# Layer 0's experts: the fifth block of 128 slots in groups of four slices, behind a jump on TensorE

## The chip, the cores and the metric

The kernel runs on one core of a Trainium2 chip. The metric is the device time of one execution in microseconds (us). A core has TensorE (PE, matrix products; its weight loads are shown as PEld), VectorE (DVE), ScalarE (ACT), GpSimd (POOL) and SyncE (SP), which run at the same time and wait for each other by semaphores. Here SP issues the plain DMA transfers and POOL the indirect ones (gathers and scatters).

## The reference

Two layers, each an attention followed by a mixture of experts, on 2048 tokens of 512 numbers. The change lies in layer 0's experts alone:

```
E, K = (NUM_EXPERTS, TOP_K)                       # 8, 2
C = math.ceil(CAPACITY_FACTOR * S * K / E)        # ceil(1.25 * 2048 * 2 / 8) = 640
probs = jax.nn.softmax(xr @ Wg, axis=-1)
gate_vals, expert_idx = jax.lax.top_k(probs, K)
...
dispatched = xr[dispatch_mask.reshape(-1) % S].reshape(E, C, d)
h = jax.nn.relu(jnp.einsum('ecd,edf->ecf', dispatched, w1))
expert_out = jnp.einsum('ecf,efd->ecd', h, w2)
```

Each of 8 experts has 640 slots. A token goes to two experts, so an expert gets 512 tokens on average, and how many it gets is known only when the router has run. An expert multiplies its slots by w1 (512 x 2048), takes the relu, and multiplies by w2 (2048 x 512). The rows go back to their tokens with their weights and are added.

## The kernel before

The program runs in stages: layer 0's attention with its router, layer 0's experts, layer 1's attention with its router, layer 1's experts. All matrix products are of 32-bit floats.

**The experts' stage** (`Experts0`). The 640 slots of an expert are five blocks of 128 (`NBLK0`), the 2048 inner columns are 16 slices of 128 (`SLICES`). `fetch` gathers a block's token rows from DRAM on POOL (g), `turn` transposes them on TensorE (tr) and copies them on DVE into xT, the expert's tokens with the 512 features on the partitions. Both are done one expert ahead, a block every two slices. Slots without a token gather some row, have the weight zero, and are scattered to rows behind the table.

For each slice, `first` computes h = w1 slice x tokens: two halves of 320 slots, each four products of 128x320 that add up in one PSUM bank (h0, h1), then a relu into hT, on ACT for the first half and on DVE for the second. `second` multiplies hT's five blocks by the slice's rows of w2, and adds them to five PSUM banks (o0 to o4) over the 16 slices. At the last slice `result` takes each o with its slots' weight into y (even blocks on ACT, odd ones on DVE), and POOL scatters y with an addition into x_dram.

`run` sets the order: for each slice `first` of this slice, then `second` of the slice before, so that the relu runs while TensorE does other products. Then come the next expert's fetch and turn, and one piece of work for layer 1 (`extra`: rope tables, and weights to load).

`weights` loads a pair of slices' w1 and w2, 512 KB each, on SP, with three buffers for each.

The compute engines keep the program's order inside this stage (`Engines`, `InOrder`); SP's transfers are placed by the framework's scheduler. The profile gives nearly all of these instructions the line of the recording helper, L65, so they are told apart by their tiles. The tiles w1 and w2 are both called w there.

[...]

## Time and profile before

| | |
|---|---|
| median of 3 runs | 3962.63 us (3961.39 to 3962.63) |
| the profiled execution | 3962.43 us |
| its span, first to last instruction | 3960.7 us |
| TensorE busy in the span | 3762.5 us |
| layer 0's experts, first h to last o on TensorE | 1413.3 to 2536.4 us |
| TensorE idle between that stage and layer 1 | 31.2 us |

In lines of groups, the part before the bar gives engine, operation, result and operands, shape and count; behind it stand busy time in all and mean duration of one, then the engine's idle time just before these instructions and what ended it. A product of 32-bit floats leaves two matmul records and two weight loads, a transpose one of each. Timeline lines give start, length and the merged instructions, in brackets the idle time before them and what ended it.

### The profile page before, as it was taken

The numbers are of one execution on the slowest core, as the hardware profiler recorded it, in microseconds if no ns is written. First come the engines' busy times: TensorE is split into PE (matmuls) and PEld (weight loads), VectorE is DVE, ScalarE is ACT, GpSimd is POOL, SyncE is SP. The second block draws the span as 40 slices with busy tenths as digits, with TensorE's granted clock in tenths as the row PEclk, the third lists the DMA queues.
The fourth block names the chain that finished last, engine by engine and source line by source line (L and its number), as shares of the span: only waits on it lengthen the run. The fifth ranks groups of instructions, "written<-read, shape, count | busy, mean of one in ns | idle before, by whom it ended". The sixth has DMA issues, their size and how long they took to land. (4 is left out here: it accounts for less than half of the span.)

```text
span 3960.7 us, 44119 instructions
## 1 busy us (share of the span) xinstructions
PE 3762.5 (95%) x14481; PEld 2417.1 (61%) x14481; DVE 1873.6 (47%) x4335; ACT 1369.1 (35%) x5089; POOL 1205.3 (30%) x1488
## 2 busy tenths in 40 slices
PE   5999899899999889999999999699999999997998
PEld 3776677688788755555555555355555555554565
DVE  7878877777788823100000000055555555553111
ACT  4665555566766401000000000043443433341111
POOL 7446655644522123111011000042222222220332
PEclk8999999899999989999999999899999999998999
DMA  5223332322322253233233232200000100005433
GB/s 170 90 94 117 115 105 95 120 91 96 115 81 81 72 191 99 93 90 82 61 91 85 65 85 72 57 22 25 28 31 22 31 22 29 18 11 207 75 65 56
DMA packets 134818, 312.45 MB, mean 79 GB/s; under 512 B 15872, under 2 KB 16000, under 8 KB 132800
## 3 DMA queue, kind: packets, MB, share of 16 engines
q1 hardware_dynamic: 116896, 268.21, 20.8%
q0 software_dynamic: 17696, 41.43, 5.7%
q8 instruction: 117, 1.92, 0.2%
q14 instruction: 109, 0.89, 0.1%
HBM read 231.72 MB, written 77.86 MB: 78 GB/s over the span
## 5 line engine op out<-in xcount | busy, mean ns | idle before, releaser
L65 PE MATMUL h<-xT,w 128*128 128x320 f32 x2048 | 574.8, 434 | 4.1 <-ACT hT L65 4.1
L65 PE MATMUL o<-w,hT 128*128 128x512 f32 x1280 | 570.0, 592 | 0.0
L65 PEld LDWEIGHTS h<-xT,w 128*128 128x128 f32 x2048 | 387.9, 191 | 191.1 <-issue 43.7
L65 DVE TENSOR_SCALAR hT<-h 128x320 f32<-128x320 f32 x128 | 62.9, 492 | 784.4 <-PE h L65 776.3
L65 PEld LDWEIGHTS o<-w,hT 128*128 128x128 f32 x1280 | 243.2, 190 | 265.5 <-issue 245.1
L65 ACT ACTIVATE hT<-h 128x320 f32<-128x320 f32 x128 | 55.8, 436 | 923.0 <-PE h L65 923.0
L65 POOL DMA_INDIRECT x_dram<-y,e_target x40 | 62.8, 1571 | 867.3 <-ACT y L65 717.4
L65 ACT ACTIVATE p<-sc,sm_nm 128x128 f32<-128x128 f32 (+1 forms) x768 | 300.9, 408 | 25.0 <-DVE sm_nm L65 14.4
L65 PE MATMUL mm<-w,xq 128*128 128x512 f32 x1024 | 294.6, 432 | 14.4 <-ACT raw L65 7.6
L65 PE MATMUL po<-w,cq 128*128 128x512 f32 x1024 | 274.2, 410 | 6.3 <-DVE cq L65 6.3
L65 PE MATMUL sc<-kT,qT 128*128 128x128 f32 (+1 forms) x1536 | 266.8, 310 | 5.9 <-ACT p L65 5.9
L65 PEld LDWEIGHTS sc<-kT,qT 128*128 128x128 f32 x1536 | 222.6, 191 | 63.2 <-issue 45.7
L65 PE MATMUL pv<-pT,v 128*128 128x256 f32 (+1 forms) x768 | 257.7, 459 | 1.4 <-ACT pT L65 1.4
L65 ACT ACTIVATE hn_sq<-mm 128x128 f32<-128x128 f32 x768 | 213.3, 278 | 121.1 <-PE mm L65 102.0
L65 DVE TENSOR_REDUCE sm_nm<-sc 128x4 f32<-128x512 f32 (+1 forms) x256 | 176.0, 687 | 140.6 <-PE sc L65 138.9
L65 PEld LDWEIGHTS mm<-w,xq 128*128 128x128 f32 x1024 | 198.8, 200 | 60.0 <-ACT raw L65 8.4
L65 PE MATMUL po<-c_wo,oT 128*128 128x512 f32 x512 | 231.4, 595 | 0.0
L65 PE MATMUL mm<-c_wq,hT 128*128 128x512 f32 x512 | 230.4, 593 | 0.4 <-DVE qn L65 0.4
L65 PEld LDWEIGHTS po<-w,cq 128*128 128x128 f32 x1024 | 185.7, 191 | 42.8 <-DVE cq L65 7.2
L65 POOL TENSOR_TENSOR hn_rs<-hn_rs,mhalf 128x4 f32<-128x4 f32 x192 | 197.2, 1027 | 16.0
L65 ACT ACTIVATE rms_sq<-mm 128x128 f32<-128x128 f32 x384 | 106.8, 278 | 273.2 <-PE mm L65 227.2
L65 PE MATMUL h<-e_w,xT 128*128 (+1 forms) x624 | 199.1, 462 | 1.7 <-DVE xT L65 1.7
(213 smaller groups left out, 6241.8 us busy)
## 6 DMA issues: line engine op xcount, KB each, us to landing
w<-in_f_w SPq DMA_DIRECT2D x128, 512.0 KB, 3.7
x_dram<-xr SPq DMA_DIRECT2D x64, 256.0 KB, 2.0
xr<-x_dram SPq DMA_DIRECT2D x64, 256.0 KB, 2.9
e_w<-in_f_w SPq DMA_DIRECT2D x8, 1408.0 KB, 22.3
xk<-in_ctxT SPq DMA_DIRECT2D x32, 256.0 KB, 2.8
xv<-in_ctxT SPq DMA_DIRECT2D x32, 256.0 KB, 3.3
raw<-in_wproj SPq DMA_DIRECT2D x32, 256.0 KB, 3.0
lnT<-kept_lnT SPq DMA_DIRECT2D x32, 256.0 KB, 3.2
```

Of the source, the lines that this page charges most:

```text
L65: return self.tc.keep_in_program_order(call(*args, **kwargs))
```

## The change

The fifth block of every expert is taken out of `first` and `second`. These now handle 512 slots: `first` makes four products of 128x512 into one bank (h), with one relu on ACT; `second` makes four products into o0 to o3.

The fifth block is done in `last`, for four slices at a time, inside a `Switch` on TensorE. For each expert TensorE has a register: 1 if slot 512 of the expert holds a token, else 0. All eight are read at the stage's start. Where it is 1, TensorE computes the block's h for the four slices of a group (hl, one bank) and the o products of the group before (ol, one bank). Where it is 0, it jumps over them. The relu of hl (rest, on DVE) and the result of ol are done either way, on what the bank holds; an empty block's weights are zero. There are five switches to an expert: four groups, and one for the last group's o products.

w1 now has 4 buffers and w2 has 6. The PSUM banks are h, hl, ol, o0 to o3 and the transposes.

In the built program the switches stand earlier than the source has them: group 0's is beside the switch that closes the expert before, inside slice 13 of that expert, and those of groups 1, 2 and 3 are inside slices 1, 7 and 11, in most experts.

```diff
     SLICES = FF0 // P
+    GROUP = 4
+    FULL = NBLK0 - 1
...
+        self.h_last = ops.t(psum, [P, self.GROUP, P], F32, "hl")
+        self.o_last = ops.t(psum, [P, D], F32, "ol")
+        ops.nc.vector.memset(self.h_last, 0.0)
+        ops.nc.vector.memset(self.o_last, 0.0)
+
+        used = ops.t(work, [P, E], I32, "used")
+        last = self.table[:, :P].rearrange("p (e b) -> p e b", e=E)[:, :, self.FULL]
+        ops.nc.vector.tensor_scalar(used, last, 0.0, None, ALU.is_gt)
+        loads, self.used = self.plain.values_load_multi_w_load_instructions(
+            used[0:1, :], engines=(mybir.EngineType.PE,), min_val=0, max_val=1,
...
-        w1 = t(self.work, [P, NC, 256], F32, "w1", 3)
+        w1 = t(self.work, [P, NC, 256], F32, "w1", 4)
...
-        w2 = t(self.work, [P, 2, D], F32, "w2", 3)
+        w2 = t(self.work, [P, 2, D], F32, "w2", 6)
...
     def first(self, e, k):
+        n = self.FULL * P
...
+        ps = self.ops.t(self.psum, [P, n], F32, "h")
+        self.inner(ps, e, k, slice(0, n))
+        hT = self.h[e, k] = self.ops.t(self.work, [P, n], F32, "hT", 3)
+        self.ops.nc.scalar.activation(hT, ps, AF.Relu)
...
+    def last(self, e, group, before):
+        g = self.GROUP
+        for arm in self.tc.Switch({mybir.EngineType.PE: self.used[e]}, 2):
+            if arm:
+                if before is not None:
+                    for i in range(g):
+                        self.outer(self.o_last, e, before * g + i, self.rest[e, before][:, i, :])
+                if group is not None:
+                    for i in range(g):
+                        s = slice(self.FULL * P, CAP)
+                        self.inner(self.h_last[:, i, :], e, group * g + i, s)
+        if group is not None:
+            rest = self.rest[e, group] = self.ops.t(self.work, [P, g, P], F32, "rest", 2)
+            self.ops.nc.vector.tensor_scalar(rest, self.h_last, 0.0, None, ALU.max)
+        else:
+            self.result(e, self.FULL, self.o_last)
...
             self.first(e, k)
             if i:
                 self.second(*steps[i - 1])
+            group, at = divmod(k, self.GROUP)
+            if at == self.GROUP - 1:
+                self.last(e, group, group - 1 if group else None)
+            if e and k == 0:
+                self.last(e - 1, None, groups - 1)
...
         self.second(*steps[-1])
+        self.last(E - 1, None, groups - 1)
```

`inner` holds the four products of `first` and `outer` the one product of `second`, on the slots they are given.

More of the change, by code (lines that the diff above doesn't have):

```diff
@@ L954 @@
     SLICES = FF0 // P
+    GROUP = 4
+    FULL = NBLK0 - 1
     def __init__(self, ops, tc, args, router, x_dram, sum_dram, work, psum):
+        self.plain, self.tc = ops.nc, tc
+        ops.nc = Engines(tc, ops.nc)
         self.ops, self.args, self.work, self.psum = ops, args, work, psum
@@ L961, in __init__ @@
         rows_behind(ops, work, sum_dram)
-        self.xT, self.g, self.w, self.h, self.outs = {}, {}, {}, {}, {}
+        self.xT, self.g, self.w, self.h, self.rest, self.outs = {}, {}, {}, {}, {}, {}
+        self.h_last = ops.t(psum, [P, self.GROUP, P], F32, "hl")
[7 more added lines that the diff above has]
+            used[0:1, :], engines=(mybir.EngineType.PE,), min_val=0, max_val=1,
+            skip_runtime_bounds_check_because="it is the result of a comparison",
+        )
+        for i in loads:
+            tc.keep_in_program_order(i)
     def column(self, e, b):
@@ L979, in weights, with inner @@
         nc, t = self.ops.nc, self.ops.t
-        w1 = t(self.work, [P, NC, 256], F32, "w1", 3)
+        w1 = t(self.work, [P, NC, 256], F32, "w1", 4)
         nc.sync.dma_start(out=w1, in_=self.args["f0_w1"][e, f])
-        w2 = t(self.work, [P, 2, D], F32, "w2", 3)
+        w2 = t(self.work, [P, 2, D], F32, "w2", 6)
         nc.sync.dma_start(out=w2, in_=self.args["f0_w2"][e, f])
         self.w[e, f] = w1, w2
+    def inner(self, ps, e, k, s):
+        w1, at = self.w[e, k // 2][0], k % 2 * P
+        for c in range(NC):
+            self.ops.nc.tensor.matmul(
+                ps, w1[:, c, at : at + P], self.xT[e][:, c, s],
+                start=(c == 0), stop=(c == NC - 1),
+            )
@@ L986, in first, with outer @@
+    def outer(self, out, e, k, hT):
+        w2 = self.w[e, k // 2][1]
+        self.ops.nc.tensor.matmul(
+            out, hT, w2[:, k % 2, :], start=(k == 0), stop=(k == self.SLICES - 1)
+        )
     def first(self, e, k):
-        nc, t = self.ops.nc, self.ops.t
+        n = self.FULL * P
         if k % 2 == 0:
             self.weights(e, k // 2)
-        w1, at = self.w[e, k // 2][0], k % 2 * P
-        hT = self.h[e, k] = t(self.work, [P, CAP], F32, "hT", 3)
-        half = CAP // 2
@@ L993, in first @@
-        for i in range(2):
-            s = slice(i * half, i * half + half)
-            ps = t(self.psum, [P, half], F32, f"h{i}")
-            for c in range(NC):
-                nc.tensor.matmul(
-                    ps, w1[:, c, at : at + P], self.xT[e][:, c, s],
-                    start=(c == 0), stop=(c == NC - 1),
-                )
-            if i:
-                nc.vector.tensor_scalar(hT[:, s], ps, 0.0, None, ALU.max)
-            else:
-                nc.scalar.activation(hT[:, s], ps, AF.Relu)
+        ps = self.ops.t(self.psum, [P, n], F32, "h")
@@ L1006, in second @@
+        self.inner(ps, e, k, slice(0, n))
+        hT = self.h[e, k] = self.ops.t(self.work, [P, n], F32, "hT", 3)
+        self.ops.nc.scalar.activation(hT, ps, AF.Relu)
     def second(self, e, k):
-        nc, t = self.ops.nc, self.ops.t
         if k == 0:
-            self.outs[e] = [t(self.psum, [P, D], F32, f"o{b}") for b in range(NBLK0)]
-        hT, w2 = self.h.pop((e, k)), self.w[e, k // 2][1]
-        for b in range(NBLK0):
-            nc.tensor.matmul(
-                self.outs[e][b], hT[:, b * P : (b + 1) * P], w2[:, k % 2, :],
-                start=(k == 0), stop=(k == self.SLICES - 1),
-            )
-            if k == self.SLICES - 1:
-                self.result(e, b)
@@ L1019, in result @@
-    def result(self, e, b):
+            self.outs[e] = [self.ops.t(self.psum, [P, D], F32, f"o{b}") for b in range(self.FULL)]
+        hT = self.h.pop((e, k))
+        for b, out in enumerate(self.outs[e]):
+            self.outer(out, e, k, hT[:, b * P : (b + 1) * P])
+            if k == self.SLICES - 1:
+                self.result(e, b, out)
+    def last(self, e, group, before):
[14 more added lines that the diff above has]
+            self.result(e, self.FULL, self.o_last)
@@ L1021, in result @@
+    def result(self, e, b, out):
         nc = self.ops.nc
@@ L1025, in result @@
         if b % 2:
-            nc.vector.tensor_scalar(y, self.outs[e][b], weight, None, ALU.mult)
+            nc.vector.tensor_scalar(y, out, weight, None, ALU.mult)
         else:
-            nc.scalar.activation(y, self.outs[e][b], AF.Copy, scale=weight)
+            nc.scalar.activation(y, out, AF.Copy, scale=weight)
         scatter_add(self.ops, self.sum_dram, self.target[:, col : col + 1], y)
@@ L1034, in run @@
             self.turn(0, b)
+        groups = self.SLICES // self.GROUP
         steps = [(e, k) for e in range(E) for k in range(self.SLICES)]
@@ L1048, in run @@
         self.second(*steps[-1])
+        self.last(E - 1, None, groups - 1)
+        self.ops.nc = self.plain
 def layer0_experts(ops, tc, args, router, x_dram, sum_dram, extra):
@@ L1054, in layer0_experts @@
         psum = ctx.enter_context(tc.tile_pool(name="b_ps", bufs=1, space=PSUM))
-        scheduled, ops.nc = ops.nc, Engines(tc, ops.nc)
         Experts0(ops, tc, args, router, x_dram, sum_dram, work, psum).run(extra(work))
-        ops.nc = scheduled
 ORDER1 = (
```

## The prediction

> **What bounds the kernel now.** I read the page's busy table first, then its groups, then TensorE's timeline inside layer 0's experts, then the table by stages, and last the queues.

> ```profile
> PE 3762.5 (95%) x14481; PEld 2417.1 (61%) x14481; DVE 1873.6 (47%) x4335; ACT 1369.1 (35%) x5089; POOL 1205.3 (30%) x1488
> ...
> q8 instruction: 117, 1.92, 0.2%
> ...
> L65 PE MATMUL h<-xT,w 128*128 128x320 f32 x2048 | 574.8, 434 | 4.1 <-ACT hT L65 4.1
> L65 PE MATMUL o<-w,hT 128*128 128x512 f32 x1280 | 570.0, 592 | 0.0
> ```

> TensorE is busy 95% of the span, and the two groups of the stage (h and o) hold 1144.8 us with 4.1 us of idle time before them. A product of 32-bit floats leaves two records: 2048 for 128 slices x 8 products. The mean durations (434, 592 ns) overlap, so I take the pace from starts.

> ```profile
> 1528.19 4.46 PE L65 MATMUL o<-w,hT 128*128 128x512 f32 x10
> 1532.49 4.47 PE L65 MATMUL h<-xT,w 128*128 128x320 f32 x16
> 1536.79 4.45 PE L65 MATMUL o<-w,hT 128*128 128x512 f32 x10
> ...
> 1579.79 4.46 PE L65 MATMUL o<-w,hT 128*128 128x512 f32 x10
> 1588.35 6.26 PE L65 MATMUL h<-xT,w 128*128 128x320 f32 x16 [4.11 <-ACT hT L65]
> ```

> A slice takes 1536.79 - 1528.19 = 8.60 us: 4.30 for h, 4.30 for o, so one o product of 512 columns costs 4.30/5 = 0.86 us. The last two lines show what an idle TensorE costs besides the gap: after 4.11 us idle the same 16 records take 6.26 us, 1.8 more than 4.47.

> ```profile
> 1690.00:1830.00 140.00, 140.00 (x439) 81.14 (x438) 12.82 (x23) 9.06 (x19) 12.70 (x10) 1.00 0.29 79
> ```

> In this stretch (columns: us, PE, PEld, DVE, ACT, POOL busy, clock, DMA share, GB/s) TensorE never rests, the clock is full, DMA is at 29%. So the stage is pure TensorE time, and matmul time taken away here leaves the end earlier, unless something new stops TensorE.

> [...] 1.92 MB / 117 = 16.4 KB; no run here shows a jump's wait. [...]

> **The change, part by part.**

> 1. *Matmuls that stay for every expert.* h becomes 4 products of 512 columns, o 4: 8 x 0.86 = 6.87 us a slice. Against 8.60 (8.594 over the 140 us stretches) that is -1.72 us, x128 = **-220**.

> 2. *Matmuls of the fifth block where it is used.* A slice costs one o product (0.86) and four of 128 columns. For these the nearest row is sc of layer 0, with the same shape:

> ```profile
> 905.26 1.06 PE L65 MATMUL sc<-kT,qT 128*128 128x128 f32 x8
> 906.08 2.11 PE L65 MATMUL po<-w,cq 128*128 128x512 f32 x8
> ```

> 8 records, 4 products, in 0.82 us (0.89 at its next place): 0.22 each, 0.88 for four. So 1.74 us a slice, and an expert that uses the block pays 6.87 + 1.74 = 8.61: nothing gained, nothing lost. How many use it is in the data: the reference's routing gives its experts 583, 588, 427, 481, 435, 542, 456 and 584 tokens, so experts 0, 1, 5 and 7 exceed 512. 4 x 16 x 1.74 = **+111**. Parts 1 and 2 together: -109.

> 3. *The switches.* 5 per expert, 40 in all, 20 taken and 20 jumped over. In the built program's order each ends a block of code; both arms stand in instruction blocks of their own. The empty arm waits until TensorE's own earlier matmuls are done, adds the count that they would have, and jumps. So it drains the array: semaphore, branch, next weight load, some 0.7 us, between 0.5 and 1. Then fetches: the nearest price is a 16 KB load, whose time from issue to landing the transfers view gives as 2.0 us (posi); a q8 packet alone is about 1.1 us (0.2% of 16 x 3961 us / 117). I take F = 2 us, with 0 and 4 as ends. *Alone* (12 jumped): the switch stands inside h of slices 1, 7 and 11. The sequencer gets there when the relu of the slice before is done, about 0.9 us after that h, while 3.44 us of o and 1.72 us of h lie in the queue: 4 us of cover. Two fetches of 2 just fit: 1.0 each, 12 us. *At borders* the last switch of an expert and the first of the next follow each other with nothing between. Jumped-jumped (2/3, 3/4): 2F+1 each; jumped-taken (4/5, 6/7): F+1; taken-jumped (1/2, 5/6): 2F-1, since four products of the taken arm cover one; taken-taken (0/1): F-0.5; the stage's start, with an empty queue: F+1; the last expert's closing switch, one h product behind the one before: F-0.5. With F = 2: 10+6+6+1.5+3+1.5 = 28. Cold clock after the two longest gaps: 2 x 1.8 = 4. Sum **+44**. Taken switches elsewhere: 0, hidden by the same queue; at 1 us each it would be 12.

> 4. *Waits on other engines.* ACT takes all 512 columns of relu: the y row of the same size is 0.69 us (2533.00 in the timeline), against 0.44. h has one PSUM buffer, and the next h comes after 3.44 us of o: hidden; were ACT late by 2.5 us, TensorE would wait. DVE gives up 128 x 0.49 us and gets 32 of about 0.75, read one switch later: hidden. The eight-register load on TensorE waits for DVE's comparison and stands before the first transposes, where TensorE is idle 6.8 us until 1403.26: 0, up to 2. Two memsets on DVE (about 0.5 each) stand behind the gather indices: 0. [...]

> 5. *Loads on SP.* w1 gets 4 buffers, w2 6. In the built order every load is behind the h or o that frees its buffer; with the durations above the shortest time from that to first use is 6 us, and 4.3 us in the last expert, against 3.7 us from issue to landing (w row, 512 KB). At the stage's start group 1 is hoisted before the second slice and wants four w1: 4 MB instead of 3 MB in the way, at 322 GB/s up to 3 us; I take 1.

> 6. *Gathers on POOL.* The five scatters of an expert are in line before the next gather: in the trace they start at 1981.39 and the gather issues at 2008.68, its transpose runs at 2018.05, some 6.5 us after the rows land if they take 2 us. Four shorter slices and a shorter o take 6.5 to 7.7 us of that: **+2** in all, from 0 to 6.

> 7. *The end.* The chain is the last expert's scatters:

> ```profile
> 2533.96 1.55 POOL L65 DMA_INDIRECT x_dram<-y,e_target  x1 [105.78 <-ACT y L65]
> ...
> 2557.02 1.56 POOL L65 DMA_INDIRECT x_dram<-y,e_target  x1 [4.94 <-issue]
> ```

> Five in 28 us, then layer 1. They hang on the first y, which keeps its place: 0.

> Sum: -220 + 111 + 44 + 1 + 2 = -62. Against the profiled execution (3962.43 us, of which 3960.7 are span; the median is 3962.63) that is **3900**.

> **The rivals.**
> - *Cheap jumps* (fetches always ahead, F near 0): 20 x 0.7 = 14 instead of 44, so 3868, range 3855 to 3878. For it: the bodies lie close behind the code. Against: nothing in the trace shows how far ahead TensorE fetches.
> - *Uncovered jumps, slower.* If a switch can only fetch once TensorE is drained, or the sequencer isn't ahead, each pays its fetches in full. The point where it decides is 109/40 = 2.7 us per switch, taken or not. At F near 4 with one fetch uncovered in each, 40 x 4 = 160: 4013. For it: the empty arm's wait is a drain. Against: the four us of queue.
> - *Nothing is jumped over.* If all eight read as used, 128 x 0.01 plus some 25 for the switches: 3989. The counts speak against it.

> **How the numbers follow.** Partly hidden fetches, 3880 to 3940: 0.60; cheap jumps 0.20; uncovered 0.12; nothing jumped over 0.03; between the first and the third, 3940 to 3970: 0.05. A measurement of this kernel can tell about 0.2%, 8 us, from no change. Faster 0.82, same 0.04, slower 0.14. The range 3858 to 3950 leaves out some 0.03 below and 0.17 above.

> **What would show it.** The h row of 128x512 with 1024 records at 430 ns, o 1024; hl with 512 records and ol with 128, which is half of what eight used experts would leave; gaps of TensorE of about 1 us, three in each unused expert, and longer ones at borders; q8 well above 117 packets; slices of 6.87 us in experts 2, 3, 4 and 6. Gaps over 3 us at the lone switches, or gaps at taken ones, would prove it wrong on the slower side; hl with 1024 records, on the data.

## The result, and the profile after

The changed kernel takes **4035.05 us** (median of four runs, 4030.42 to 4038.11) against 3962.63: a ratio of 1.0181 [1.0163, 1.0198], 72 us slower. The prediction was 3900 us.

The page's busy table and groups of the changed kernel, beside those shown of before:

```profile
PE 3701.5 (92%) x13841; PEld 2274.6 (56%) x13841; DVE 1831.0 (45%) x4242; ACT 1386.4 (34%) x5089; POOL 1205.4 (30%) x1488
...
q8 instruction: 225, 3.69, 0.4%
...
L65 PE MATMUL h<-xT,w 128*128 128x512 f32 x1024 | 491.9, 621 | 93.6 <-issue 92.8
L65 PE MATMUL o<-w,hT 128*128 128x512 f32 x1024 | 466.8, 599 | 0.0
```

The two new groups, from the view of groups in this stage:

```profile
L65 PE MATMUL hl<-xT,w 128*128 128x128 f32 x512 | 67.3, 296 | 23.8 <-issue 23.8
L65 PE MATMUL ol<-w,rest 128*128 128x512 f32 x128 | 63.4, 642 | 20.8 <-DVE rest L65 15.8 <-issue 4.9
```

TensorE has less to do, as meant: 640 records fewer, and hl and ol have half of what eight used experts would leave. TensorE's busy time fell by 61 us, but the span grew by 76 (4036.4 against 3960.7), so the rest is idle time. Before, h and o had 4.1 us of it in front of them. Now the four groups have 93.6 + 23.8 + 20.8 = 138.2 us. The second part of the bill is slower products: the mean of an h record is 621 ns, where the same work without switches has 596 (shown below).

The waits of TensorE in the stage (columns: total us, times, longest) say what ended those gaps:

```profile
PE h L65 <- issue: 92.8, 16, 12.4
PE hl L65 <- issue: 23.8, 4, 9.0
PE ol L65 <- DVE rest L65: 15.8, 1, 15.8
PE ol L65 <- issue: 4.9, 2, 2.7
```

"issue" means that TensorE waited for nothing that the profile shows. Its timeline at one jumped switch (one whose register is 0; expert 2, group 1):

```profile
1738.66 3.60 PE L65 MATMUL o<-w,hT 128*128 128x512 f32 x8
1742.09 1.88 PE L65 MATMUL h<-xT,w 128*128 128x512 f32 x4
1748.21 2.85 PE L65 MATMUL h<-xT,w 128*128 128x512 f32 x4 [4.24 <-issue]
1750.85 4.48 PE L65 MATMUL o<-w,hT 128*128 128x512 f32 x8
```

There are 4.24 us without a matmul, and the next eight o records take 4.48 instead of 3.60: the clock granted to TensorE was 1.00 in the gap, 0.67 on average from 1750 to 1754 us, and 1.00 again in the four us behind. The view by source line shows what TensorE's sequencer, which hands it its instructions, did during the gap. A switch has two jumps, one into an arm (the entering jump) and one out of it (the leaving jump). This is the line of the switch's branches in that window (columns: shortest/median/longest in ns, first and last start):

```profile
L1654 PEldq COMPARE_BRANCH  x2: 322/2156/3991, 1739.8 to 1744.2; - x2
```

The entering jump took 0.32 us, while 4 us of products were queued. The leaving jump, out of the empty arm, began at 1744.2, when the array had just drained (finished all products given to it), and took 3.99 us. That is the gap. In these 3.99 us the instruction queue (q8) moved one packet of 16 KB, which began 1.64 us after the jump and took 0.97 us.

The switches that jump explain 110.8 us of the idle time: twelve lone gaps of 3.65 to 5.16 (52.7 in all), at switches with products on both sides, and six at borders between experts, where two switches stand back to back (58.1). A border where both switches jump:

```profile
1859.87 3.78 PE L65 MATMUL h<-xT,w 128*128 128x512 f32 x4 [12.40 <-issue]
```

### The profile page after: what moved, and what is told of

Same layout as the page of the kernel before. It is cut to its first block, busy times and chain, and to the rows that moved or that the text cites. A ratio compares the mean times of both kernels' runs of the same rounds, so it can differ in the third digit from the quotient of the medians.

```text
span 4036.4 us, 43072 instructions
## 1 busy us (share of the span) xinstructions
PE 3701.5 (92%) x13841; PEld 2274.6 (56%) x13841; DVE 1831.0 (45%) x4242; ACT 1386.4 (34%) x5089; POOL 1205.4 (30%) x1488
## 3 DMA queue, kind: packets, MB, share of 16 engines
q8 instruction: 225, 3.69, 0.4%
## 5 line engine op out<-in xcount | busy, mean ns | idle before, releaser
L65 PE MATMUL h<-xT,w 128*128 128x512 f32 x1024 | 491.9, 621 | 93.6 <-issue 92.8
L65 PE MATMUL o<-w,hT 128*128 128x512 f32 x1024 | 466.8, 599 | 0.0
L65 ACT ACTIVATE hT<-h 128x512 f32<-128x512 f32 x128 | 76.3, 596 | 1035.4 <-PE h L65 1035.4
L65 PEld LDWEIGHTS h<-xT,w 128*128 128x128 f32 x1024 | 195.9, 197 | 328.2 <-issue 326.6
L65 DVE COPY xT<-tr 128x512 f32<-128x512 f32 x79 | 54.3, 688 | 671.8 <-PE tr L65 671.8
L65 PEld LDWEIGHTS o<-w,hT 128*128 128x128 f32 x1024 | 199.4, 195 | 254.8 <-issue 254.5
L65 POOL DMA_INDIRECT x_dram<-y,e_target x40 | 62.8, 1571 | 908.0 <-ACT y L65 769.4
L65 PE MATMUL mm<-w,xq 128*128 128x512 f32 x1024 | 296.9, 434 | 15.5 <-DVE xq L65 7.8
L65 ACT ACTIVATE p<-sc,sm_nm 128x128 f32<-128x128 f32 (+1 forms) x768 | 300.1, 407 | 24.8 <-DVE sm_nm L65 14.1
L65 PE MATMUL po<-w,cq 128*128 128x512 f32 x1024 | 274.3, 410 | 6.2 <-DVE cq L65 6.2
L65 PE MATMUL sc<-kT,qT 128*128 128x128 f32 (+1 forms) x1536 | 266.8, 310 | 6.0 <-ACT p L65 6.0
L65 PE MATMUL pv<-pT,v 128*128 128x256 f32 (+1 forms) x768 | 257.5, 459 | 1.3 <-ACT pT L65 1.3
L65 PEld LDWEIGHTS sc<-kT,qT 128*128 128x128 f32 x1536 | 222.7, 191 | 63.2 <-issue 45.4
L65 ACT ACTIVATE hn_sq<-mm 128x128 f32<-128x128 f32 x768 | 212.9, 277 | 121.0 <-PE mm L65 102.4
L65 DVE TENSOR_REDUCE sm_nm<-sc 128x4 f32<-128x512 f32 (+1 forms) x256 | 175.9, 687 | 140.8 <-PE sc L65 138.9
L65 PEld LDWEIGHTS mm<-w,xq 128*128 128x128 f32 x1024 | 200.7, 202 | 61.5 <-ACT raw L65 8.6
L65 PE MATMUL po<-c_wo,oT 128*128 128x512 f32 x512 | 231.4, 595 | 0.0
L65 PE MATMUL mm<-c_wq,hT 128*128 128x512 f32 x512 | 230.4, 593 | 0.4 <-DVE qn L65 0.4
L65 PEld LDWEIGHTS po<-w,cq 128*128 128x128 f32 x1024 | 185.8, 191 | 42.7 <-DVE cq L65 7.1
L65 POOL TENSOR_TENSOR hn_rs<-hn_rs,mhalf 128x4 f32<-128x4 f32 x192 | 198.6, 1034 | 16.0
L65 PE MATMUL h<-e_w,xT 128*128 (+1 forms) x624 | 200.3, 465 | 1.7 <-DVE xT L65 1.7
L65 ACT ACTIVATE rms_sq<-mm 128x128 f32<-128x128 f32 x384 | 106.6, 278 | 274.9 <-PE mm L65 221.4
```

Of the source, the lines that this page charges most:

```text
L65: return self.tc.keep_in_program_order(call(*args, **kwargs))
```

## The experiments

**Theory T.** A jumped switch costs what its leaving jump takes: the code behind the switch is not loaded, its fetch starts only once TensorE has drained, and a slow clock follows. Pairs at borders pay most. Taken switches are nearly free, because their own products cover their jumps. A jump that waits for such a fetch of its own is called missed below. **Rivals:** the drain and the semaphore wait themselves; the regrouping and the taken arms; matmuls that shrank less than worked out. Ratios are to the kernel before, run on the same chip; differences in us from the changed kernel are from its 4035.05.

### No switch at all: what the matmuls are worth

```diff
-        for arm in self.tc.Switch({mybir.EngineType.PE: self.used[e]}, 2):
+        for arm in (int(e in (0, 1, 5, 7)),):
```

> No switch at all: which experts compute the fifth block is fixed when the kernel is built (0, 1, 5 and 7), and the fifth block of experts 2, 3, 4 and 6, which holds no token, is left out. Buffers, relus, results and groups are those of the changed kernel. Theory T: the matmuls saved (109 us) come in full, what remains is at most the wait of ol for rest (16 to 18 us): 3962 - 109 + 18 = 3871 us, between 3850 and 3880. Rival M (the saving in matmuls is smaller than worked out): above 3900. Rival O (the other engines, whose work is the same here, hold TensorE up by themselves): above 3900 with gaps that end on ACT or DVE.

Measured: 3850.88 us against 3966.46, ratio 0.9709 [0.9692, 0.9725], -116 us. Its groups in the stage:

```profile
L65 PE MATMUL h<-xT,w 128*128 128x512 f32 x1024 | 463.3, 596 | 3.9 <-ACT hT L65 3.9
L65 PE MATMUL o<-w,hT 128*128 128x512 f32 x1024 | 460.3, 592 | 0.0
L65 PE MATMUL hl<-xT,w 128*128 128x128 f32 x512 | 59.7, 275 | 0.0
L65 PE MATMUL ol<-w,rest 128*128 128x512 f32 x128 | 57.5, 592 | 0.0
```

The saving is real, and the other engines, with the same work, don't hold TensorE up. The time is 20 us below theory T's 3871, because the wait for rest is gone here too. These four rows are also the yardstick for the changed kernel. Its groups are 1089.4 us busy where these are 1040.8: 48.6 us more for the same products. They have 138.2 us of idle time where these have 3.9: 134.3. Together that is 183, against 178.7 between the two profiled spans. The clock records tell where the 48.6 us come from: each of the twelve lone gaps and six border gaps counted above is followed by products at half the clock, or runs into such a stretch (3.4 to 13.7 us each). So **a quarter of the loss is the clock after the gaps**.

### All experts take the full arm: what taken switches cost

```diff
-        ops.nc.vector.tensor_scalar(used, last, 0.0, None, ALU.is_gt)
+        ops.nc.vector.tensor_scalar(used, last, 0.0, None, ALU.is_ge)
```

> The comparison for the register is 'at least 0', so all eight experts run through the full arm: 40 switches, none jumped over, the fifth block computed for every expert as in the kernel before. Theory T: taken switches cost next to nothing, what is left is the wait of ol for rest (15.8 us in the changed kernel), the start (some 7 us), 7 borders at about 2 us: 3962 + 1 + 16 + 2 + 7 + 14 = 4002 us, between 3985 and 4015. Rival R (taken arms and regrouping cost as much as jumped ones): 20 more taken arms add to the changed kernel's 4035 at least the 109 us of their matmuls: 4100 to 4150. Rival M (the matmuls did not shrink): near 4035.

Measured: 4036.61 us, ratio 1.0178 [1.0161, 1.0195], 35 us above theory T's number, outside its range, and far below rival R's. It is near rival M's number, but the kernel without switches rules M out. The lone taken switches cost nothing, as the timeline shows; at the end of this stretch stands a border:

```profile
1676.66 1.88 PE L65 MATMUL h<-xT,w 128*128 128x512 f32 x4
1678.38 3.60 PE L65 MATMUL ol<-w,rest 128*128 128x512 f32 x8
1681.81 3.73 PE L65 MATMUL hl<-xT,w 128*128 128x128 f32 x32
1685.38 1.88 PE L65 MATMUL h<-xT,w 128*128 128x512 f32 x4
...
1708.04 4.13 PE L65 MATMUL hl<-xT,w 128*128 128x128 f32 x22 [4.89 <-issue]
```

The jump into this lone arm took 3.32 us (the longer of the two branches in the source view), and no product was held up:

```profile
L1654 PEldq COMPARE_BRANCH  x2: 332/1826/3320, 1674.0 to 1683.4; - x2
```

A missed jump was therefore harmless under queued products. What T had too small were the borders: six of the seven show gaps of 4.6 to 5.3 us, since the closing arm's four products cannot cover the jumps of two switches. The products behind these gaps are slower, too: hl takes 131.8 us, where twice the 59.7 above would be 119.4.

### The empty arm last

```diff
-        ops.nc.vector.tensor_scalar(used, last, 0.0, None, ALU.is_gt)
+        ops.nc.vector.tensor_scalar(used, last, 0.0, None, ALU.is_le)
...
-            if arm:
+            if not arm:
```

> Only the two arms change places: the register is 1 where the expert has no token in the fifth block, and the full arm is the first body, so that the empty arm stands right in front of the code behind the switch. The same matmuls, waits and drains are left. Theory T (the empty arm's leaving jump goes to a block that is not resident, and its fetch starts only once TensorE has drained, some 4 us, with some 2 us of slow clock behind it): the 12 lone jumped switches leave gaps under 1.5 us instead of 3.65 to 5.16, the four borders with a jumped switch lose 3 to 8 us each, and the time is 3937 us, between 3915 and 3955. Rival D (the drain and the semaphore wait of the empty arm cost the gap, wherever its code lies): gaps stay near 4 us, 4035 us, above 4020. Rival R (the regrouped work of the taken arms and the wait for rest hold the loss): 4030 to 4040.

Measured: 4001.45 us, ratio 1.0095 [1.0078, 1.0112]. Rival D is out, for drains and waits are the same and 34 us are gone. But T expected 98, almost three times that. The gaps of groups 2 and 3 fell to about 2, those of group 1 stayed near 4.8, and borders with two jumped switches stayed above 11:

```profile
1741.32 3.31 PE L65 MATMUL h<-xT,w 128*128 128x512 f32 x4 [4.76 <-issue]
1818.22 1.98 PE L65 MATMUL h<-xT,w 128*128 128x512 f32 x4 [1.99 <-issue]
1843.94 3.78 PE L65 MATMUL h<-xT,w 128*128 128x512 f32 x4 [11.28 <-issue]
```

The records of the sequencer and of the instruction queue tell more. Behind the entering jump, at the start of every arm, stands an instruction BRANCH_PREFETCH_HINT (the hint). The changed kernel's trace has 40, one per switch, and behind 34 of them a q8 packet began 0.60 to 0.72 us later. At the gap that ends at 1818.22 the entering jump began at 1811.67 and took 3.35 us; the hint was followed, some 0.7 us later, by a fetch of 1.02 us, so part of it lay ahead of the leaving jump (1816.50, 1.67 us). At 1741.32 the hint stood only 0.85 us ahead of the leaving jump, and the fetch came 2.1 us after that jump began. So with this order the fetch can start early, and **how much is queued at the switch** seems to decide how early; the last two kernels test this.

### The border's two switches apart

```diff
-            group, at = divmod(k, self.GROUP)
-            if at == self.GROUP - 1:
+            if k in (3, 7, 11, 14):
+                group = (3, 7, 11, 14).index(k)
...
+                if k in (4, 6, 10, 12, 14):
+                    self.turn(e + 1, (4, 6, 10, 12, 14).index(k))
```

> Arms as in the changed kernel. Only the places of two turns and of group 3 differ: the transposes of block 2, 3 and 4 of the next expert come at slices 10, 12 and 14, group 3 is emitted at slice 14. In the built order the switch that closes an expert then stands in slice 13 and the next expert's first group in slice 15, two slices apart instead of back to back. Theory T with the pair as a cost of its own (the second switch of a pair has no queued matmul in front of it and pays both its jumps in the open): each border with a jumped switch falls to the price of lone switches (4 us and 2 us of slow clock each): jumped-taken and taken-jumped from some 9.5 to 6.3, jumped-jumped stays near 12.6; with the seventh closing switch 4015 us, between 4000 and 4028. Rival: the pair costs no more than its two switches by themselves: 4035, within 6 us. In both cases lone gaps stay at 3.6 to 5.2 us.

Measured: 4015.90 us, ratio 1.0127 [1.0110, 1.0144]: T's 4015. The border of 12.40 us is now two gaps:

```profile
1842.41 3.22 PE L65 MATMUL h<-xT,w 128*128 128x512 f32 x4 [3.93 <-issue]
1861.94 5.30 PE L65 MATMUL h<-xT,w 128*128 128x512 f32 x6 [4.25 <-issue]
```

Back to back, the second switch finds the queue empty, and both its jumps are in the open: at that border of the changed kernel they took 3.11 and 4.48 us, and the first of them began 4.45 us after the last product had ended.

### The wait for rest

```diff
-            if i >= 4 and extra:
+            if i >= 4 and extra and not 15 <= i <= 20:
```

> The changed kernel, with no step of the other work of this stage (rope and the like, on DVE, ACT and POOL) handed in at the steps 15 to 20; it follows six steps later. Theory Q: the one long wait of ol for rest in expert 1 (15.8 us and some 2 us of slow clock behind it) comes from rest standing on DVE behind rope work that waits for POOL, which is at its five scatters: it goes or shrinks to under 4 us, and the time falls by 14 to 18, to 4018 us, between 4010 and 4026. Rival: the pile-up moves with the work, or another wait ends at the same time: 4035, within 6 us.

Measured: 4016.91 us, ratio 1.0129 [1.0112, 1.0146], 18 us less than the changed kernel: theory Q. No wait of ol for rest is left among TensorE's waits. The changed kernel's timeline shows the chain:

```profile
1604.99 0.31 ACT L65 ACTIVATE rp_o<-rp_a 128x128 f32<-128x128 f32 x1 [16.75 <-POOL rp_r L65]
1605.53 1.45 DVE L65 TENSOR_SCALAR rp_n<-rp_n 128x128 f32<-128x128 f32 x1 [18.24 <-ACT rp_n L65]
...
1607.81 0.68 DVE L65 TENSOR_SCALAR rest<-hl 128x512 f32<-128x512 f32 x1
1608.54 3.78 PE L65 MATMUL ol<-w,rest 128*128 128x512 f32 x4 [15.79 <-DVE rest L65]
```

The relu of hl takes 0.68 us, but it is in line behind a rope step that waits for ACT, which waits for POOL. The kernel before had this pile-up too: there ACT waited 15.96 us for POOL's rp_r, and hT, in line behind, held TensorE up for the 4.11 us that the prediction shows.

### One switch per border

```diff
-        for arm in self.tc.Switch({mybir.EngineType.PE: self.used[e]}, 2):
+        border = group == 0 and e > 0
+        if border:
+            before = self.SLICES // g - 1
+        owner, n = (e - 1, 4) if border else (e, 2)
+        used = self.used[E + e - 1] if border else self.used[e]
+        for arm in self.tc.Switch({mybir.EngineType.PE: used}, n):
```

> Arms in the changed kernel's order, but the switch that closes an expert and the next expert's first group are one switch of four arms (nothing, ol, hl, both), on a register that holds used[e] + 2 * used[e+1]: 33 switches instead of 40. Theory P (the second switch of a pair pays its jumps in the open): the two borders with nothing on either side fall from some 14 us to one lone jump (6), the four with work on one side from 10 to 11 us to about 1, since taken switches with queued matmuls around them are free: -16 - 38 = -54, 3981 us, between 3968 and 3993. Rival: a switch costs the same wherever it stands, 72 + 109 = 181 us over 40, 4.5 each, so seven fewer save 32: 4003. Rival: the table of four arms has a price of its own: above 4010.

Measured: 3971.88 us, ratio 1.0015 [1.0009, 1.0022]: -63 us against the changed kernel, where T had -54. Borders with work on one side are down to 1.4 to 1.5 us, those without are one lone gap (4.14 and 3.90). The wait for rest also fell here, from 15.8 us to 6.4, which is about the surplus:

```profile
PE ol L65 <- DVE rest L65: 6.4, 1, 6.4
```

### These edits together

> Three edits on the changed kernel together: one switch per border with four arms, the empty arm as the last body of every switch, and no rope work at the steps 15 to 20. If they add up: 3981 for the merged borders, -16 for the wait of ol for rest, and for the arms' order at the lone switches of groups 2 and 3 (8 times some 2.3 us of gap and 1 of slow clock) -26: 3939 us, between 3925 and 3953, which is below the kernel before. If the order of the arms only paid at borders (which are gone): 3965. What stays by theory T: 4 gaps of 4.8 us at group 1, 10 of 2 to 3.

Measured: 3910.13 us, ratio 0.9854 [0.9832, 0.9875]: 29 us better than the sum of 3939, outside its range. Part of the surplus lies at group 1. With the merged border its switch stands in the middle of the o products, with more in the queue, and its gap in expert 2 is down to 0.67 us (4.24 in the changed kernel; "<-PEq" is a wait that TensorE's sequencer ended):

```profile
1716.16 3.60 PE L65 MATMUL h<-xT,w 128*128 128x512 f32 x8
1719.59 1.88 PE L65 MATMUL o<-w,hT 128*128 128x512 f32 x4
1722.14 1.98 PE L65 MATMUL o<-w,hT 128*128 128x512 f32 x4 [0.67 <-PEq L1052]
```

This suggested the last pair of kernels, where this one is called e8_best.

### A short full arm: does distance matter

The full arm holds four hl products, and the rest of the fifth block is left out.

> Arms in the changed kernel's order; the full arm is cut to four hl products (of one slice), so most of the fifth block's work is left out for all experts, and the empty arm has only some 16 instructions to jump over instead of about 80. The taken arms do 20 x 0.9 = 18 instead of 111 us: -93. Theory T1 (the leaving jump misses because it is a jump that isn't to the next instruction, near or far): lone gaps stay at 3.6 to 5.2 us and the time is 3945, between 3935 and 3965. Rival L (it misses because the target lies too far behind, outside what is loaded): lone gaps fall under 1 us and the time is near 3830.

A single run: 4000.13 us. The lone gaps of experts without work stay (3.6 to 5.0, one of 6.5), though only some 16 instructions are jumped over: T1, not L as it was put. But the records do not show where the arms lie in memory, so few instructions in between need not mean that the target was near. The number itself was missed by 55 us, outside T1's range. The trace shows 40 us more idle time of the groups than in the changed kernel, and h alone 20 us busier. A part of this supports the theory of cover: a taken arm with 0.9 us of products no longer hides its own two jumps. At one taken switch, in the source view and in the timeline:

```profile
L1654 PEldq COMPARE_BRANCH  x2: 3300/3510/3719, 1654.4 to 1658.6; - x2
```

```profile
1658.77 1.05 PE L65 MATMUL hl<-xT,w 128*128 128x128 f32 x8
1661.97 1.98 PE L65 MATMUL h<-xT,w 128*128 128x512 f32 x4 [2.15 <-issue]
```

### More in the queue at the switch, and the same with the old order of arms

```diff
             self.outer(out, e, k, hT[:, b * P : (b + 1) * P])
...
+            if b == 1 and turn:
+                self.turn(*turn)
```

> The kernel of e8_best, with the transposes of the next expert's block put between the second and the third o product of a slice instead of behind the fourth. In the built order most switches then stand between o3 of one slice and h of the next (or in the middle of the o products) instead of inside h, so TensorE has some 7 us of issued products in its queue when its sequencer reaches the switch, instead of some 5. Theory T (the price of a jumped switch is the time from the drain to the arrival of the code behind it; with the empty arm last its fetch begins some 0.7 us after the hint at the arm's start, and the code is there some 6 us after the first jump begins): the gaps of the lone jumped switches fall from 2 to 4 us to under 1 us, as at the group-1 switches of e8_best, and the slow clock behind them goes too: 3878 us, between 3860 and 3893. Rival (the drain sets the gap, or the jump costs its time wherever it starts): gaps stay at 2 to 4 us, 3910 within 6 us.

> The kernel of e10_mid with the arms in the order of the changed kernel: the empty arm first, the full arm between it and the code behind the switch. Theory T (here the leaving jump's fetch starts only after the drain, however early the arm was entered): gaps of 3.3 to 5.5 us at all 14 jumped switches, each with 1 to 2 us of slow clock: 14 x 5.5 = 77 above a kernel without gaps, 3945 us, between 3930 and 3960. Rival C (only the queued products at the switch matter, not the order of the arms): within 8 us of e10_mid.

Measured: **3875.87 us**, ratio 0.9784 [0.9767, 0.9800], with the empty arm last (e10_mid), where theory T had 3878 and e8_best took 3910.13; 3964.68 us, ratio 1.0006 [0.9998, 1.0015], with it first, 20 us above theory T's number and 5 above its range, but far from rival C's. The place of the switches is the same in both, and the arms' order alone is worth 89 us. The waits of h's products on the code behind a switch, with the empty arm last:

```profile
PE h L65 <- issue: 9.4, 5, 4.1
PE h L65 <- PEq L1054: 6.3, 9, 0.9
```

One jumped switch of that kernel, in the timeline and in the source view:

```profile
1750.05 1.88 PE L65 MATMUL o<-w,hT 128*128 128x512 f32 x4
1752.59 3.70 PE L65 MATMUL h<-xT,w 128*128 128x512 f32 x8 [0.66 <-PEq L1054]
```

```profile
L1662 PEldq COMPARE_BRANCH  x2: 409/2058/3706, 1745.7 to 1752.1; - x2
```

The same views of one with the empty arm first:

```profile
1787.51 1.88 PE L65 MATMUL o<-w,hT 128*128 128x512 f32 x4
1793.24 3.08 PE L65 MATMUL h<-xT,w 128*128 128x512 f32 x4 [3.85 <-issue]
```

```profile
L1661 PEldq COMPARE_BRANCH  x2: 325/1963/3601, 1783.1 to 1789.6; - x2
```

Empty arm last: the long jump (3.71) comes first, while products run, and the leaving jump takes 0.41. Empty arm first: the short one is first, and the long one (3.60) comes after the drain. The drain where the leaving jump is short costs 0.66 us, all told; the prediction's estimate was 0.7. Over all 14 jumped switches the leaving jumps took 0.40 to 1.89 us with the empty arm last and 3.60 to 5.89 with it first. The kernel with the empty arm last is 2.2% faster than before and 0.8% from the one without switches; the difference in idle time (20.7 against 3.9 us) and in busy time (1053.5 against 1040.8) of the four groups, 29.5 us, accounts for it.

## Why the prediction was wrong

The chance of slower was put at 0.14. That outcome came, on the mechanism of the rival "uncovered jumps", though not as that rival had it: its 40 switches at 4 us were to pay whether taken or not, and it put the decision at 2.7 us per switch. Most of the loss came from the 20 jumped ones (110.8 of 138.2 us idle), and lone taken ones paid nothing but at the stage's start and end. The sign that the prediction named for this side, gaps over 3 us at the lone switches, is what came.

**Parts 1 and 2, right.** -109 was worked out, -116 measured without switches. Four used experts, 512 hl and 128 ol records, 6.87 us a slice: as stated. Only the sign "1024 records at 430 ns" mixes two things: 430 ns is the time from start to start, and the view's mean is 596 even without switches, as it was 592 for the o records before.

**Part 3, the step that failed**, +44 against some 165 (the 183 above, less 18 for rest). Three of its terms were wrong:
- *"Two fetches of 2 just fit"* in 4 us of queue. The prediction itself says that the empty arm waits for the array before it jumps, and then lets the fetch of that jump run under the queue all the same. That TensorE's sequencer gets to the switch with 4 us of products still queued was the author's estimate, and the trace has it: at the jumped switch shown above the entering jump began at 1739.8 us, and the last product ended at 1744.0. But at the twelve lone gaps the leaving jump began after the drain, and its fetch 0.9 to 2.5 us later. The entering jump took 0.31 to 0.33 us in eleven of the twelve. So the lone gaps were 4.4 us on average, not 1.0: 52.7 instead of 12.
- *F = 2 us*, priced by the loads and the packet. The packet did take 0.9 to 1.4 us in most cases, but a missed jump took 3.3 to 4.9 us in most: 0.9 us or more until the fetch began, and some 1.4 behind the packet until the jump was over. How long the fetch waited went with the other DMA traffic: in the changed kernel's missed jumps, second switches of pairs aside, 0.97 us in the middle case of 16 (0.89 to 1.11) where other packets took under 10% of the DMA engines meanwhile, and 1.64 in that of 15 (0.96 to 3.69) where they took over 30%. No run changes that traffic alone, so this is not shown as a cause. The prediction's upper end of 4 was the better guess. At borders this gave 11.7 and 12.4 instead of 5, about 9 instead of 3 before a used expert, about 8 instead of 3 after one: 58.1 where these six had 22. The stage's start, the border of experts 0 and 1 and the last switch together took 10.7 instead of 6.
- *"Cold clock after the two longest gaps"*, 4 us. Every gap of some 4 us and more had its slow stretch: 48.6 us in all, some 2 of them behind the wait for rest. The 6.26 us line shown before was about the price, to be paid some twenty times.

That a jump waits for a fetch was an assumption of the prediction, and its price an estimate. The changed kernel's trace shows the wait: the instruction queue moved a packet during 48 of TensorE's 80 jumps, and 43 of these took 3.28 us or more. Of the 32 others 31 took 0.31 to 0.42. Whether the distance of the jump matters is not shown: the one over some 16 instructions missed all the same, but nothing shows where its target lay.

**Part 4, wrong in one place.** ACT's relu took 596 ns and was hidden, and the 40 branches on each of the other engines cost nothing (0.03 to 0.05 us each). But "read one switch later: hidden" counted only rest's own time, not what stands ahead of it on an engine that works in order: 15.8 us and the clock after it, 18 by the run that takes it away.

**Parts 5, 6 and 7, not at fault.** No load or gather shows among the waits that grew, and TensorE's wait between the stage and layer 1 is 32.2 us where it was 31.2.

**The weighing.** "If a switch can only fetch once TensorE is drained" stood in the text as the condition of the slower rival. Its 4013 and the forecast's 3900 differ in F and in what the queue covers (and in 3 us for the loads and gathers, which the rivals leave out), and the trace of the kernel before shows no such jump to choose by. A chance of 0.12 was too small for a case that nothing on the page excluded.

Left open is why, with the empty arm first, the fetch that follows its hint did not serve the leaving jump (3.60 to 5.89 us in the last kernel), although the hint there stood 6 to 7 us ahead of that jump at twelve of the fourteen jumped switches. The records show when a fetch ran, not what it brought, and no run tests it.

## What to carry to other kernels

What paid here: price a branch on TensorE by what is still queued when its fetch starts, put the arm without work last (89 us here), stand the switch where several microseconds of products have just been issued, and merge switches that would stand back to back (63 us). An arm that drains the array leaves nothing to hide the jump behind it: at the twelve lone gaps of the changed kernel the leaving jump began 0.19 us after the last product had ended, and took 3.4 to 4.9. A gap of some 4 us was paid twice, as idle time and as slow clock (4.24 us, and then 4.48 instead of 3.60 for eight o records). Shorter gaps often were not: behind the gap of 1.99 us shown above four h records took 1.98 us, against 1.88 without a gap. A small step moved to an engine that works in order inherits everything in line ahead of it there, as rest did: 0.68 us of work, and 15.79 us of TensorE's time waiting for it.
